# A graph network's last half: layer input added by TensorE, scaling split over two engines, h in one piece, new ranks

## The chip, the cores and the metric

One of the eight cores of a Trainium2 chip runs the kernel. A core has TensorE (matrix products into PSUM), VectorE, ScalarE and GpSimd (which work on SBUF, the first two on PSUM too), and SyncE, whose queue issues most of the transfers. In the profile they are PE (PEld for its weight loads), DVE, ACT, POOL and SP. Each engine takes its own instructions in program order; semaphores hold an instruction until what it reads is there. The metric is the device time of one execution in microseconds, median of three runs; less is better.

## What is computed

Sixteen images of 1024 nodes with 128 features (`x`), and one symmetric 0/1 matrix `adj`. A graph attention layer and a residual norm, then five steps of a gated graph network and another residual norm:

```python
# layer 0
h = x @ others_weight
e = leaky(u1[idx1] + u2[idx2])                 # one logit per pair
att = softmax(where(adj > 0, e, NEG_BIG), axis=1)
x = layernorm(x + att @ h + x @ self_weight)
# layer 1, five steps from h = x
m = adj @ h                                    # in and out matrix are the same
u = h @ u3.T
z = sigmoid([m, m] @ w3.T + b3 + u)
r = sigmoid([m, m] @ w4.T + b4 + u)
hv = tanh([m, m] @ w5.T + b5 + (r * h) @ u5.T)
h = (1 - z) * h + z * hv
# and the end
out = layernorm(x + h)                         # x: what entered layer 1
```

## The kernel before

**Tiles and stages.** An image's state lies transposed, features on the partitions and nodes along the row, in two halves of 512 nodes (`hT`, half 0 and 1). Images are taken in pairs, 0 and 1 up to 14 and 15. `layer0(b)` makes an image's layer input `y0`, stores a copy in DRAM (`yd`) for the end, and starts `hT`. `messages(q, s, k)` multiplies a pair with the adjacency matrix in step `s`: every operand is split into a high and a low part in a rounded fp32 format (`split`, L603 on ScalarE and L607 on VectorE), and each part multiplied (`product`, L615). Most steps share seven block products between the pair's two images; the first three steps of the first pair and the last three of the last pair are "plain" (`PLAIN`), image by image.

**A step of a gate.** `gates(b, s, soon)` handles both halves `e`: the product of `u3` with h (L1186), its copy (L1189), the products for r and z added in PSUM (L1196), their activations (L1199, a tanh from which the sigmoid is made), r times h (L1206), two products for the new value (L1212, L1213), tanh (L1221), and three VectorE instructions: hv minus h (L1224), times z (L1227), h (L1230). `pieces(b, s)` says in how many column pieces the part from the tanh on is done: 2 of 256 columns in the last step of the last image, otherwise 1 of 512.

**The end of an image.** `leave(b, s)` follows. After the last step each half is turned back to nodes on partitions: for the last three images by TensorE (`transposes`, L565, four 128x128 transposes), for the others by VectorE and transfers. The layer input comes back from DRAM (L1286), VectorE adds it (L1297), and `layernorm` does the rest: VectorE takes the statistics in four pieces of 128 (L521, L523), GpSimd makes 1/sqrt(var + eps) by a power (L527, L528), and then there are two forms. The long form has GpSimd make a bias too (two more instructions, L533 and L534 or L536 and L537) and ScalarE scale (L542, four instructions). The short form has VectorE subtract and multiply (L548, four instructions). The short form is used for the last image and for the second half of the image before it. Images 0 to 13 are stored through GpSimd's queue, the last two through SyncE's (L1317).

**The order of the work.** No loop sets it. Each piece of work is entered with `plan.add(engine, length, rank, ...)`, with what it reads and writes. `Plan.order()` plays the plan through once, before the kernel is built: an engine that is free takes the ready piece of lowest rank for which the tiles are free. A piece is ready when those before it have ended plus a lag by engine (`LAG`), and `CARE` ns more where VectorE or ScalarE feeds TensorE. Lengths on VectorE and ScalarE count 1.1 times (`MARGIN`). What comes out is emitted as it stands, so that ranks and lags decide the order of the instructions and nothing at run time.

A rank is mostly `rank_of(b, s)`: 10 for each pair, 4.2 for each step, and `LATER` for the last image in its plain steps. To this comes an offset by kind of work out of the table `D`: `pu`, `u`, `pr`, `pz`, `r`, `pv`, `z`, `hv`, `h` for the parts of a step, `m` for copies of messages, `tr` for turning back, `o`, `ln`, `out` for the end. `rank0(b)` with `l1` to `l8` is the same for the parts of layer 0: `l1` projections, `l2` row sums, `l3` scaled operands, `l4` products, `l5` turning, `l6` norm, `l7` and `l8` what follows.

**The start.** While `adj` is loaded TensorE runs up to 120 filler transposes (L419, rank 9000). Then come the projections of images 0 and 1 (L652), the row sums of the exponentials (L807, VectorE), the scaled operands (L856 ScalarE, L862 VectorE) and the attention products (L615 into `ps_acc_po`). For images 4 to 7 the product of `x` with the residual weights is made early (L455, "ahead", copied by L458 and stored). From image 2 on a row of exponentials goes through DRAM and comes back spread over all partitions (`pb`, L701 and L708).

Of the kernel before, what the change touches and what calls it, by code (L numbers as in the profile page):

```python
# [13 lines left out]
ALU = mybir.AluOpType  # L14
AX = mybir.AxisListType

P = 128
# [3 lines left out]
STEPS = 5  # L21
# [4 lines left out]
LOW, HIGH = -20.0, 100.0  # L26
TINY = 1e-30
PLAIN = {(0, 0), (0, 1), (0, 2), (7, 2), (7, 3), (7, 4)}
LATER = 3
AHEAD = range(4, 8)  # L30
LATE = 3001
TURNED = {(0, 0), (0, 1), (7, 2), (7, 3)}
# [3 lines left out]
class Plan:  # L36
# [5 lines left out]


    MARGIN = 1.1
    CARE = 200
    SAME = {"PE": 0, "DVE": 60, "ACT": 60, "POOL": 60, "SP": 2500, "DMA": 0}
    LAG = {"PE": 250, "DVE": 150, "ACT": 170, "POOL": 200, "SP": 2500, "DMA": 2400}

# [25 lines left out]
    def order(self):  # L74
# [14 lines left out]
        while events:  # L89
# [13 lines left out]
            while more:  # L103
                more = False
                for engine, queue in ready.items():
# [3 lines left out]
                    while queue:  # L109
# [3 lines left out]
                        if all(free[t[0]] > 0 for t in new):  # L113
# [6 lines left out]
                            for u in users[i]:  # L120
# [3 lines left out]
                                if ops[u][0] == "PE" and engine in ("DVE", "ACT"):  # L124
                                    lag += self.CARE
                                at[u] = max(at.get(u, 0), now + length + lag)
# [11 lines left out]
def kernel(  # L138
# [51 lines left out]
    nc = tc.nc  # L190
    B = x_t.shape[0]
# [15 lines left out]
    ident = const.tile([P, P], F32, tag="ident", name="ident")  # L207
# [10 lines left out]
    def exact(pools):  # L218

        def pool(name, bufs, space=None):  # L220
# [34 lines left out]
            "rstd": (3, [P, 2, 4], F32, None),  # L255
            "D": (6, [P, HALF], F32, bass.MemoryType.DRAM),
            "X": (24, [P, HALF + 16], F32, bass.MemoryType.DRAM),
# [9 lines left out]
        def T(t, dtype=None, shape=None):  # L267
            if t not in tiles:
                _, sh, dt, _ = kinds[t[0]]
                tiles[t] = places[t[0]].tile(  # L270
                    shape or sh, dtype or dt, tag=t[0], name="_".join(map(str, t)).replace("-", "n")
                )
            return tiles[t]
# [8 lines left out]
        def chunks(ap):  # L282

            return ap.rearrange("p (b c i) -> p c b i", b=4, c=4)

        plan = Plan({tag: k[0] for tag, k in kinds.items()})

        R, F, TR, V, A = 233, 858, 109, 605, 640

        def pe(*a, **k):  # L290
            plan.add("PE", *a, **k)

        def dve(*a, **k):
            plan.add("DVE", *a, **k)
# [4 lines left out]
        def sp(*a, **k):  # L299
            plan.add("SP", *a, **k)  # L300


        D = dict(m=-0.2, pu=1.4, u=0.8, pr=0.8, pz=1.4, r=1.7, pv=1.2, z=1.3, hv=-0.6, h=1.2, tr=1.6, o=5.0, ln=2.9)
        D.update(out=4.8, l1=-9, l2=-4, l3=-3, l4=-4, l5=-6, l6=-2.5, l7=-1, l8=-2)

        def on_pe(b, what):

            return b < 2 and what in ("y", "b") or b >= B - 3 and what == STEPS - 1 or (b // 2, what) in TURNED

        def plain(q, s):  # L310

            return (q, s) in PLAIN

        def rank_of(b, s):
            return 10 * (b // 2) + 4.2 * s + (LATER if b == B - 1 and plain(b // 2, s) else 0)

        def rank0(b):
            return 10 * (b // 2) - 1 * (1 - b % 2) + -1.0

        def sign(b):  # L320

            return 1 if b % 2 else -1
# [17 lines left out]
        def early_loads():  # L340
# [28 lines left out]
            writes=[(boot, "early"), (ws, "early"), (x0, "early"), (("xt", 1), "early"), *((t, "early") for k in staged for t in k)],  # L369
# [190 lines left out]
        def transposes(src, read, t, rank, cs=range(4), part=0):  # L560


            def emit():
                for j in cs:
                    nc.tensor.transpose(T(t)[:, j * P : (j + 1) * P], src()[:, j * P : (j + 1) * P], ident)  # L565

            pe(len(cs) * TR, rank, emit, reads=[*read, (("ident",), 0)], writes=[(t, part)])

        def turn(t, src, read, rank):


            def emit():
                nc.vector.transpose(T(t).rearrange("p (b c i) -> p b c i", b=4, c=4), turned(src()))

            dve(V, rank, emit, reads=read, writes=[(t, 0)])
# [49 lines left out]
        def layer0(b):  # L625

            first = rank0(b) - (60 if b == 0 else 0)
            rank = first + D["l1"]
            xt, hx, pb, u, us, uu, ud = (
# [147 lines left out]

            rank = first + D["l2"]

# [19 lines left out]

            rank = rank0(b) + D["l2"]  # L800
            junk = ("junk", b)
# [42 lines left out]
            if b == 0:  # L844
                own_weights()
            rank = rank0(b) + D["l3"]
            size = 1 if b == 0 else 4
# [317 lines left out]

        def pieces(b, s):

            return 2 if b == B - 1 and s == STEPS - 1 else 1

        def gates(b, s, soon):  # L1170
            rank = rank_of(b, s)
# [4 lines left out]
            for e in range(2):  # L1176
# [40 lines left out]
                for i in range(n):  # L1217
# [23 lines left out]
                    dve(length, rank + D["h"], times_, reads=[(hv, 1, i), (z, 1)], writes=[(hv, 2, i)])  # L1241
                    dve(length, rank + D["h"], h_, reads=[(hv, 2, i)], writes=[(hT, e) if n == 1 else (hT, e, i)])

        def leave(b, s):

            rank = rank_of(b, s)
            hT = ("hT", b)
            for g in range(2):

                def h(g=g):  # L1250
                    return T(hT)[:, g * HALF : (g + 1) * HALF]

                k, d = ("T", b, s, g), ("X", b, s + 1, g)
                if s < STEPS - 1 and on_pe(b, s):
                    t = ("ps", "t", b, s, g)
                    transposes(h, [(hT, g)], t, rank + D["tr"])
                    split(
                        ("blk", b, "h", s + 1, g),
                        lambda t=t: T(t).rearrange("p (c a j) -> p c a j", c=4, a=4),
                        [(t, 0)],  # L1260
                        rank_of(b, s + 1),
                    )
                    continue
                if s < STEPS - 1:
                    turn(k, h, [(hT, g)], rank + D["tr"])
                    away(k, d, rank + D["tr"])
                    continue

                t = ("ps", "t", b, s, g)
                n = pieces(b, s)  # L1270
                done = [(hT, g)] if n == 1 else [(hT, g, i) for i in range(n)]
                if on_pe(b, s):
                    for i in range(n):
                        transposes(h, [done[i]], t, rank + D["tr"], range(4 * i // n, 4 * (i + 1) // n), i)
                else:
                    t = ("F", b, s, g)
                    turn(k, h, [(hT, g)], rank + D["tr"])
                    away(k, d, rank + D["tr"])
                    back(d, t, rank + D["o"])


                o, yd = ("y0" if b == B - 1 else "o", b, "o", g), ("yd", b, g)
                sp(
                    450,
                    rank + (D["o"] if b < B - 1 else 0),
                    lambda o=o, yd=yd: nc.sync.dma_start(T(o).rearrange("p c d -> p (c d)"), T(yd)),  # L1286
                    reads=[(yd, 0), (hT, g) if b < B - 1 else (("m", b, s, 0), 0)],
                    writes=[(o, "y")],
                    lag=2300,
                )  # L1290
                for i in range(n):

                    def last(i=i, t=t, o=o, flat=on_pe(b, s)):
                        cs = slice(4 * i // n, 4 * (i + 1) // n)
                        x = T(o)[:, cs, :].rearrange("p c (a j) -> p c a j", a=4)
                        v = T(t).rearrange("p (c a j) -> p c a j", c=4, a=4) if flat else chunks(T(t))
                        nc.vector.tensor_tensor(x, v[:, cs], x, ALU.add)  # L1297

                    dve(V / n, rank + D["o"], last, reads=[(t, i), (o, "y")], writes=[(o, "raw", i)])

                def at(j, o=o):
                    return T(o)[:, j, :]

                layernorm(
                    ("o", b),
                    g,
                    rank + D["ln"],
                    [(o, "raw", i) for i in range(n)],
                    at,
                    at,  # L1310
                    (o, 0),
                    sign(b),
                    b == B - 1 or b == B - 2 and g,
                )

                def out_(o=o, g=g, by=nc.gpsimd if b < B - 2 else nc.sync):
                    by.dma_start(out[b].rearrange("(c p) d -> p c d", p=P)[:, 4 * g : 4 * g + 4, :], T(o))  # L1317

                if b < B - 2:
                    plan.add("POOL", 900, rank + D["out"], out_, reads=[(o, 0)], writes=[((o, "sent"), 0)], lag=2600)  # L1320
                else:
                    sp(450, rank + D["out"], out_, reads=[(o, 0)])


        def look_at(i):
# [53 lines left out]
        for i in range(2 * NC):  # L1379
# [6 lines left out]
            reads=[  # L1386
                *((("seen",), b, k) for b in range(B) for k in range(2)),
                *((("count",), i) for i in range(2 * NC)),
                (("bad",), 0),
                (("bad",), 1),  # L1390
            ],
            writes=[(("rstd", "ends"), 0)],
# [6 lines left out]
            reads=[(("ps", "t", "flag"), 0)],  # L1399
            writes=[(("flag",), 0)],  # L1400
# [208 lines left out]
    with ExitStack() as pools:  # L1609
        exact(pools)  # L1610
# [51 lines left out]
```

## Time and profile before

| | us |
|---|---|
| median of 3 runs | 1460.12 (1458.28 to 1460.99) |
| the profiled execution | 1457.82 |
| its span | 1456.0 |

Busy time by engine, in parts of the end of the span (from the view by stretches of time):

| stretch, us | TensorE | VectorE | ScalarE | GpSimd |
|---|---|---|---|---|
| 1431 to 1436 | 5.00 | 2.72 | 3.42 | 2.84 |
| 1436 to 1441 | 5.00 | 3.40 | 3.19 | 0.84 |
| 1441 to 1446 | 1.81 | 5.00 | 0.84 | 0.00 |
| 1446 to 1451 | 0.00 | 3.78 | 0.00 | 2.63 |
| 1451 to 1456 | 0.00 | 0.00 | 0.00 | 0.00 |

In the order of time, the last instructions of the last image are: its last gate product at 1440.04, tanh in pieces from 1439.38 to 1441.94, three VectorE instructions for each of four pieces, two transposes for each piece (1441.50 to 1445.62), the adds, the statistics of half 0 (1445.04) and half 1 (1446.40), GpSimd twice two instructions (1446.26 and 1447.70), the scalings (1447.65 and 1449.19), and the two stores (issued from 1448.79 on).

The profile gives start and duration of each instruction; matmul ends are modelled, so that a group's duration is some 0.16 us longer than its spacing. Busy shares are of the span. The chain of waits is of no use here: it ends after three pieces.

### The profile page before, as it was taken

Reading aid. Unit: us, or ns where it says so; the run is one execution under the profiler, and the core shown is the slowest. Engines: PE = TensorE matmul, PEld = TensorE weight load, DVE = VectorE, ACT = ScalarE, POOL = GpSimd, SP = SyncE. Lnnn points to the kernel's source line nnn. Section 1 sums busy time; section 2 is a strip of 40 time slices with the busy share of each in tenths; the row PEclk is TensorE's granted clock in tenths of the full one; section 3 lists DMA queues with packets and bytes.
Section 4 is the critical chain, followed back from the end, with each engine's and each line's share of the span. In section 5 each row is a group of like instructions: output and inputs, shape, how many; then the busy total and the mean of one; then the engine's idle time right before and its main releaser. Section 6 shows DMA issues by size and latency. Waiting matters only on the chain. (4 is left out here: it accounts for less than half of the span.)

```text
span 1456.0 us, 17810 instructions
## 1 busy us (share of the span) xinstructions
PE 1437.2 (99%) x5020; PEld 899.1 (62%) x5020; DVE 1166.5 (80%) x2769; ACT 896.2 (62%) x1786; POOL 196.7 (14%) x320
## 2 busy tenths in 40 slices
PE   9999999999999999999999999999999999999996
PEld 7666666666666666665666566665666656556663
DVE  6886789979898788978888688887889876776445
ACT  5655665666656765756756676566665666664643
POOL 0202000112111120112201120020210112000201
PEclk9999999999999999999999999999999999999998
DMA  7305434554335543454334543455433553223201
GB/s 258 128 27 152 145 95 138 157 183 131 95 116 153 160 130 94 137 153 131 99 110 133 150 142 84 116 147 171 110 100 104 141 162 110 60 71 87 72 0 31
DMA packets 188032, 174.20 MB, mean 120 GB/s; under 512 B 34239, under 2 KB 137366, under 8 KB 187926
## 3 DMA queue, kind: packets, MB, share of 16 engines
q1 hardware_dynamic: 182562, 156.41, 37.9%
q0 software_dynamic: 4800, 15.73, 3.3%
q8 instruction: 41, 0.67, 0.2%
q10 hardware_dynamic: 564, 0.85, 0.2%
q14 instruction: 65, 0.53, 0.1%
HBM read 95.68 MB, written 77.24 MB: 119 GB/s over the span
## 5 line engine op out<-in xcount | busy, mean ns | idle before, releaser
L1212 PE MATMUL ps_g_v<-m,wm 128*128 128x512 f32 x320 | 163.4, 592 | 0.0
L1213 PE MATMUL ps_g_v<-r,u5h 128*128 128x512 f32 x320 | 163.4, 592 | 0.0
L1196 PE MATMUL gz<-m,wm 128*128 128x512 f32 x320 | 158.8, 592 | 0.0
L1196 PE MATMUL ps_g_r<-m,wm 128*128 128x512 f32 x320 | 158.6, 593 | 0.2
L1186 PE MATMUL ps_g_r<-hT,u 128*128 128x512 f32 x320 | 151.8, 592 | 0.0
L1206 DVE SCALAR_TENSOR_TENSOR r<-r,hT 128x512 f32<-128x512 f32 x160 | 108.8, 685 | 51.8 <-ACT r L1199 51.1
L615 PE MATMUL ps_acc_a<-tab,blk_s 128*128 128x512 f32 x544 | 144.6, 407 | 0.0
L1199 ACT ACTIVATE r<-ps_g_r,bh 128x512 f32<-128x512 f32 x160 | 109.5, 687 | 49.6 <-PE ps_g_r L1196 47.3
L1224 DVE TENSOR_TENSOR hv<-hv,hT 128x512 f32<-128x512 f32 (+1 forms) x162 | 109.7, 679 | 37.2 <-ACT hv L1221 36.2
L615 PE MATMUL ps_acc_po<-adj,blk 128*128 128x512 f32 x512 | 136.9, 415 | 0.3 <-DVE blk L862 0.3
L1199 ACT ACTIVATE z<-gz,bh 128x512 f32<-128x512 f32 x160 | 109.8, 687 | 24.3 <-PE gz L1196 23.6
L615 PEld LDWEIGHTS ps_acc_a<-tab,blk_s 128*128 128x128 f32 x544 | 100.8, 188 | 31.5 <-issue 6.2
L615 PEld LDWEIGHTS ps_acc_po<-adj,blk 128*128 128x128 f32 x512 | 95.7, 188 | 33.3 <-issue 9.4
L1189 ACT COPY gz<-ps_g_r 128x512 f32<-128x512 f32 x160 | 91.4, 572 | 34.8 <-PE ps_g_r L1186 33.3
L1227 DVE SCALAR_TENSOR_TENSOR hv<-z,hv 128x512 f32<-128x512 f32 (+1 forms) x162 | 108.1, 671 | 1.5 <-ACT z L1199 0.7
L1230 DVE SCALAR_TENSOR_TENSOR hT<-hv,hT 128x512 f32<-128x512 f32 (+1 forms) x162 | 108.0, 671 | 1.2
L1213 PEld LDWEIGHTS ps_g_v<-r,u5h 128*128 128x128 f32 x320 | 60.6, 189 | 76.7 <-issue 61.6
L1196 PEld LDWEIGHTS gz<-m,wm 128*128 128x128 f32 x320 | 60.6, 190 | 75.7 <-issue 75.6
L607 DVE TENSOR_TENSOR blk_s<-G,blk_s 128x512 fp32r<-128x512 f32 x136 | 91.3, 681 | 13.6 <-ACT blk_s L603 13.2
L527 POOL TENSOR_SCALAR rstd_y<-mv_y 128x4 f32<-128x4 f32 x32 | 13.2, 413 | 650.3 <-DVE mv_y L523 649.6
L603 ACT CAST blk_s<-G 128x512 fp32r<-128x512 f32 x136 | 82.0, 618 | 27.5 <-DVE G L1077 26.3
L615 PE MATMUL ps_acc<-adj,blk_h 128*128 128x512 f32 x384 | 97.5, 406 | 0.3 <-DVE blk_h L607 0.3
(189 smaller groups left out, 2586.7 us busy)
## 6 DMA issues: line engine op xcount, KB each, us to landing
G<-X SPq DMA_DIRECT2D x140, 256.0 KB
X<-T SPq DMA_DIRECT2D x552, 64.0 KB
yd<-y POOLq DMA_DIRECT2D x32, 256.0 KB, 3.0
o_o<-yd SPq DMA_DIRECT2D x30, 256.0 KB
D_y<-T_y SPq DMA_DIRECT2D x112, 64.0 KB
F_y<-D_y SPq DMA_DIRECT2D x28, 256.0 KB
X<-y SPq DMA_DIRECT2D x28, 256.0 KB
D_b<-T_b SPq DMA_DIRECT2D x112, 64.0 KB
```

Of the source, the lines that this page charges most:

```text
L607: lambda: nc.vector.tensor_tensor(half(1), src(), half(0), ALU.subtract),
L615: nc.tensor.matmul(T(bank), T(blk)[:, k, c, :], right(c), start=(first and i == 0), stop=(last and i == len(terms) - 1), skip_group_check= ...
L1186: nc.tensor.matmul(T(pr), u3, h(), start=True, stop=True)
L1189: nc.scalar.copy(T(pz), T(pr))
L1196: nc.tensor.matmul(T(p_), wm[:, j, :], T(m), start=False, stop=True, skip_group_check=True)
L1199: nc.scalar.activation(T(t), T(p_), AF.Tanh, bias=bh[:, j : j + 1], scale=0.5 * sg)
L1206: lambda r=r, h=h: nc.vector.scalar_tensor_tensor(T(r), T(r), 1.0, h(), ALU.add, ALU.mult),
L1212: nc.tensor.matmul(T(pv), wm[:, 2, :], T(m), start=True, stop=False)
L1213: nc.tensor.matmul(T(pv), u5h, T(r), start=False, stop=True)
L1224: nc.vector.tensor_tensor(T(hv)[:, w], T(hv)[:, w], h()[:, w], ALU.subtract)
L1227: nc.vector.scalar_tensor_tensor(T(hv)[:, w], T(z)[:, w], 1.0, T(hv)[:, w], ALU.add, ALU.mult)
L1230: nc.vector.scalar_tensor_tensor(h()[:, w], T(hv)[:, w], 0.5, h()[:, w], ALU.mult, ALU.add)
```

## The change

In the last step of the last two images `leave` hands over to a new function `end`, and the rest of `leave` loses its cases for them. For the very last half (image 15, half 1) TensorE first copies the layer input into PSUM by a product with the identity and then adds h's four transposed blocks to it, as plain products with the identity; statistics and the short form then read PSUM. For the other three halves the transposes and VectorE's add stay, and the long form with ScalarE is used. `pieces` always gives 1, so the last image's tanh, its three VectorE instructions and the adds work on whole halves. The layer inputs of image 14 are loaded as early as those of image 15. `LATER` goes from 3 to 1.5 and `CARE` from 200 to 400; eight entries of `D` differ; and layer 0 of images 2 and 3 has its rank lowered by 6.

```diff
-    LATER = 3
+    LATER = 1.5
-    CARE = 200
+    CARE = 400
-        D = dict(m=-0.2, pu=1.4, u=0.8, pr=0.8, pz=1.4, r=1.7, pv=1.2, z=1.3, hv=-0.6, h=1.2, tr=1.6, o=5.0, ln=2.9)
-        D.update(out=4.8, l1=-9, l2=-4, l3=-3, l4=-4, l5=-6, l6=-2.5, l7=-1, l8=-2)
+        D = dict(m=-0.4, pu=1.4, u=1.2, pr=0.8, pz=1.4, r=1.7, pv=1.0, z=1.3, hv=-0.6, h=1.6, tr=1.6, o=5.8, ln=2.9)
+        D.update(out=4.4, l1=-9, l2=-4, l3=-3, l4=-4, l5=-7, l6=-1.5, l7=-1, l8=-2)
         def rank0(b):
-            return 10 * (b // 2) - 1 * (1 - b % 2) + -1.0
+            return 10 * (b // 2) - 1 * (1 - b % 2) + -1.0 - 6 * (b // 2 == 1)
         def pieces(b, s):
-            return 2 if b == B - 1 and s == STEPS - 1 else 1
+            return 1
+        def end(b, s, g, h, rank):
+            hT, t = ("hT", b), ("ps", "t", b, s, g)
+            o, yd = ("y0" if b == B - 1 else "o", b, "o", g), ("yd", b, g)
+            sp(450, rank, lambda: nc.sync.dma_start(T(o).rearrange("p c d -> p (c d)"), T(yd)),
+                reads=[(yd, 0), (("m", b, s, 0), 0)], writes=[(o, "y")], lag=2300)
+            def y_():
+                nc.tensor.matmul(
+                    T(t), ident, T(o).rearrange("p c d -> p (c d)"), start=True, stop=False, skip_group_check=True
+                )
+            def h_():
+                for j in range(4):
+                    c = slice(j * P, (j + 1) * P)
+                    nc.tensor.matmul(T(t)[:, c], h()[:, c], ident, start=False, stop=j == 3, skip_group_check=True)
+            if (b, g) == (B - 1, 1):
+                pe(F, rank + D["tr"] + 0.1, y_, reads=[(o, "y"), (("ident",), 0)], writes=[(t, "y")])
+                pe(F, rank + D["tr"], h_, reads=[(hT, g), (t, "y"), (("ident",), 0)], writes=[(t, 0)])
+                sum_ = (t, 0)
+            else:
+                transposes(h, [(hT, g)], t, rank + D["tr"])
+                def add_():
+                    x = T(o).rearrange("p c d -> p (c d)")
+                    nc.vector.tensor_tensor(x, T(t), x, ALU.add)
+                dve(V, rank + D["o"], add_, reads=[(t, 0), (o, "y")], writes=[(o, "raw")])
+                sum_ = (o, "raw")
+            def src(j):
+                return T(t)[:, j * P : (j + 1) * P] if sum_[0] == t else T(o)[:, j, :]
+            def dst(j):
+                return T(o)[:, j, :]
+            layernorm(("o", b), g, rank + D["ln"], sum_, src, dst, (o, 0), sign(b), b == B - 1 and g == 1)
+            sp(450, rank + D["out"],
+                lambda: nc.sync.dma_start(out[b].rearrange("(c p) d -> p c d", p=P)[:, 4 * g : 4 * g + 4, :], T(o)),
+                reads=[(o, 0)])
...
+                if b >= B - 2:
+                    end(b, s, g, h, rank)
+                    continue
...
-                layernorm(
-                    ("o", b), g, rank + D["ln"],
-                    [(o, "raw", i) for i in range(n)], at, at, (o, 0), sign(b),
-                    b == B - 1 or b == B - 2 and g,
-                )
+                layernorm(("o", b), g, rank + D["ln"], (o, "raw"), at, at, (o, 0), sign(b))
```

## The prediction

> **What bounds the kernel now.** I read the page's busy shares first, then busy time by stretches of 40 us, then what TensorE waited for, then the order of time at both ends.
>
> ```profile
> PE 1437.2 (99%) x5020; PEld 899.1 (62%) x5020; DVE 1166.5 (80%) x2769; ACT 896.2 (62%) x1786; POOL 196.7 (14%) x320
> ```
>
> TensorE is busy 99% of the span. A busy TensorE can still hide gaps, so I checked the spacing: a 128x512 fp32 product starts 0.86 us after the one before it throughout, and the stretches show no holes in the middle (columns: PE, PEld, DVE, ACT, POOL busy time, clock, DMA share, GB/s).
>
> ```profile
> 0.00:40.00 40.00, 36.42 (x233) 28.62 (x234) 25.94 (x92) 20.09 (x56) 0.81 (x9) 1.00 0.73 242
> 40.00:80.00 40.00, 38.59 (x181) 28.31 (x180) 33.27 (x121) 24.38 (x64) 10.33 (x20) 1.00 0.41 133
> 80.00:120.00 40.00, 40.00 (x144) 25.53 (x144) 36.09 (x109) 24.68 (x58) 2.50 (x5) 1.00 0.12 34
> ...
> 160.00:200.00 40.00, 39.68 (x147) 25.39 (x146) 33.12 (x82) 23.03 (x44) 0.00 (x0) 1.00 0.38 103
> ...
> 1440.00:1456.00 16.00, 2.81 (x11) 0.99 (x9) 9.74 (x40) 1.06 (x3) 2.63 (x4) 0.68 0.18 54
> ```
>
> From 80 to 1440 us the missing TensorE time is 0.6 us in all (0.32 of it at 160 to 200). So the middle is TensorE's sum of work, which the change hardly touches, and time can be won or lost in three places: the first 60 us, a stall that a new order puts into the middle, and the last 16 us. In the first 60 us the stall that the new ranks can reach is the one around 50 us (order of time: start, duration, engine, line, in brackets the idle time before and what ended it):
>
> ```profile
> 47.56 1.51 ACT L542 ACTIVATE y<-ps_t_y,rstd_y 128x128 f32<-128x128 f32 x4
> 50.45 1.38 PE L565 MATMUL ps_t_b<-ident,y 128*128 128x128 f32 x4 [1.00 <-ACT y L542]
> 54.64 1.90 PE L615 MATMUL ps_acc_po<-adj,blk 128*128 128x512 f32 x7 [0.33 <-DVE blk L862]
> ```
>
> From 48.6 to 56.4 us the starts of TensorE's instructions leave 3.2 us unused (7.8 us, in which stand 8 transposes of 0.11 and 16 products of 0.234). The end:
>
> ```profile
> 1440.04 1.02 PE L1213 MATMUL ps_g_v<-r,u5h 128*128 128x512 f32 x2
> 1445.18 0.44 PE L565 MATMUL ps_t<-ident,hT 128*128 128x128 f32 x2 [1.23 <-DVE y_o L1297]
> 1447.18 0.36 DVE L523 BATCH_NORM_AGGREGATE mv_o<-stats_o 128x2 f32<-128x6 f32 x4
> 1448.12 1.04 POOL L528 TENSOR_TENSOR rstd_o<-rstd_o,mhalf 128x4 f32<-128x4 f32 x1
> 1449.19 1.12 DVE L548 TENSOR_SCALAR y_o<-y_o,mv_o,rstd_o 128x128 f32<-128x128 f32 x4 [0.43 <-POOL rstd_o L528]
> ```
>
> TensorE leaves its last gate product at E = 1440.04 + 0.86 = 1440.90. VectorE then works through 256-column pieces to 1447.54, GpSimd needs 1.6 us, VectorE's last scaling ends at 1450.31, that is E + 9.41. The store takes the other 5.7 us to 1456.0.
>
> [...] back to back the pieces start every 0.34 us and whole ones every 0.61, so halving buys overlap and costs some VectorE time. [...] the trace shows each engine in program order, so a late instruction delays all behind it. [...] a 128-column transpose here takes one record of 0.11 us, the plain fp32 product of the same size (L750) two records of 0.11, so the ratio in this trace is two.
>
> **The change, part by part.** Times in the tail are relative to E; the order on each engine is that of the changed kernel as built.
>
> 1. The layer input of the very last half goes through TensorE: one 128x512 fp32 product with the identity (as L1186: 0.86 us) stands between the last two h products and the gates. TensorE's line from the last adjacency product to E is full before (1431.8 to 1440.9 for ten products of 0.86 and one transposition group of 0.44), so nothing hides it: **+0.86**. Its input is loaded well before (the two loads are issued at 1365 in the profile), and it waits for nothing.
>
> 2. ScalarE gets the scaling of both halves of image 14 and the first of image 15 (L542, 4 pieces, 1.56 us) in place of VectorE's 1.11. Order on ScalarE: r, r, z, scale 14/0, z, tanh 0, scale 14/1, tanh 1, scale 15/0. The second z is available at -3.23 but starts after scale 14/0, at -1.9; tanh 0 then starts at -1.27 where its bank was ready at -1.52; scale 14/1 runs -0.64 to 0.92, so tanh 1 waits from 0.20 to 0.92. GpSimd's rstd for both halves (4 instructions each, 2.3 us as at 45.95 to 48.28) is done by -2.6, so these scalings wait for nothing else.
>
> 3. h in one piece. Dependent VectorE steps of 512 columns start 0.73 to 0.79 apart (1414.49, 1415.22, 1416.01). Half 0: -0.54, 0.19, 0.98 to 1.67. VectorE is in that chain until 0.98 + 0.6, so tanh 1, ready at 1.61, costs only a few hundredths: minus, times of half 1 at 1.66 and 2.4; then the layer-input add of half 0 at 3.0 (transposed by 2.35); h of half 1 at 3.6 to 4.3. Statistics of half 0: 4.25 to 5.4.
>
> 4. The last half: four plain fp32 products onto the layer input, 8 records of 0.11 = 0.87, from 4.37, readable at 5.45; statistics from PSUM (0.8 + 0.36, as L521 on ps_t_y) to 6.6. The add of 0.39 and the wait for it are gone. But GpSimd now computes four instructions for half 0 (5.47 to 7.5: 1.4 for the first two as at 1446.26 to 1447.61, then 0.3 and 0.24) where the short form had two, and the last half's two stand behind them: 7.5 to 8.95 instead of 6.7 to 8.15. That is 0.8 us of a new wait, 1.1 if the four take 2.3. VectorE scales from PSUM 9.0 to 10.1. Against 9.41: **+0.7**. The store of the last half is the same; that of half 0 (after ScalarE, 9.2) is now 0.9 ahead of it instead of 1.6, and both still overlap only in part: 0 to 0.2, taken as 0.
>
> 5. Ranks. Up to the product at 35.34 us TensorE's list is the same but for where four filler transposes stand. After it, image 2's eight projections come first (1.78 us), ending the list before the transposition of y at 48.7 instead of 48.6. There the wait for L542 is longer, since L542 now stands behind all six copies of the ahead products: 49.5 to 51.05, then the split (0.6 ScalarE, 0.65 VectorE) before the first adjacency product, 51.65 and 52.3. The list as far as 55.86 holds 4.18 us of work in 7.14: 3.0 us lost against 3.2: **-0.2**. From there I followed VectorE's list to 97 us against TensorE's: image 1's split is ready at 74.15 where it is wanted at 74.4, the next at 79.2 against 80.2, r of image 0 at 94.2 against 96.4. VectorE is nearly without a gap, but TensorE isn't held.
>
> 6. CARE 400 makes the planner put 0.2 us more between VectorE or ScalarE and TensorE. It can't gain more than the 0.6 us missing in the middle; bounds -0.6 and, if a new order meets a late transfer, several us. In the built order of the last 100 us no split, gate or copy has less TensorE work before its use than in the old one by a margin that matters (r to its product: 3.4 us at least, 1.7 needed). I take **-0.4**.
>
> Sum: 0.86 + 0.7 - 0.2 - 0.4 = **+0.96**. The profiled execution took 1457.82 (1456.0 of span), 2.3 below the median of the three runs, 1460.12; the difference is carried to the median: 1461.1.
>
> **Rivals.** (A) The early stretch holds TensorE: slower. The changed VectorE list has a row sum over image 2's exponentials (L807) ahead of image 0's split. Its operand comes through a copy at 43.4, a store, and a 512 KB broadcast behind two other transfers on SP's queue; if that lands after 49.8 us, VectorE stops and each us passes to TensorE, which has nothing else at 51. For: VectorE is busy 36 of 40 us at 80 to 120, and my comparison leaves it 0.2 to 2 us of lead to 97 us. Against: the planner allowed 3 us for that transfer, as my timing does. With 4 us more it gives 0.96 + 3.8 = +4.8, 1464.9. It decides from about 2 us on. (B) All goes well: the stall at 50 us vanishes (-3.2), the middle's too (-0.6), and the tail ends at 9.3 because GpSimd's halves fall apart: 0.86 - 0.1 - 3.2 - 0.6 = -3.0, 1457.1. Against: the longer wait for L542 is in the list. (C) The end's add on TensorE costs more than it says: TensorE rests 2.2 us before the last products, and the clock is 0.50 in the profile once it has rested (1446 to 1451). At half speed they take 1.74: +0.9, 1462.0.
>
> **Numbers.** 0.2% is 2.9 us, about what a measurement of this kernel can tell from no change. Forecast 0.56 (own range 1459.3 to 1463), A 0.30, B 0.08, C 0.06. With the forecast's edges: faster 0.10, same 0.57, slower 0.33. Low 1457.4 leaves some 0.08 under it, high 1466 about 0.12 over it.
>
> **What would show it.** In the profile after: TensorE's last gate product some 0.4 to 0.9 us later than 1440.0; a scaling of ScalarE between the last two tanh; GpSimd's last pair waiting behind four; VectorE's last scaling about 10.1 us behind E; 39.7 or more of 40 us of TensorE in each stretch from 80 to 1440. Wrong would be: a wait of TensorE for VectorE, or of VectorE for the broadcast, of over 1 us between 49 and 130 us (A), no stall near 50 us (B), or a tail that ends under 9.4 or over 11 us after E.

## The result

| | before | after |
|---|---|---|
| median, us | 1460.26 (18 runs) | 1465.32 (18 runs) |
| the profiled execution, us | 1457.82 | 1464.59 |
| its span, us | 1456.0 | 1462.4 |
| TensorE's last gate product ends (E) | 1440.90 | 1447.04 |
| VectorE's last scaling ends | E + 9.41 | E + 10.29 |

After against before: ratio 1.0033, 95% interval 1.0024 to 1.0041. The change makes the kernel slower by some 5 us. The range on record holds 1465.3, but not through its sum: that gave 1461.1, with an own range that ends at 1463, and the likeliest outcome, no difference that can be measured, did not come.

The question is where the 6.1 us that E comes later are from. First the view by stretches of time of the kernel after (columns as before: PE, PEld, DVE, ACT, POOL busy time, clock, DMA share, GB/s):

```profile
80.00:120.00 40.00, 40.00 (x147) 25.66 (x146) 35.45 (x105) 24.04 (x59) 6.73 (x14) 1.00 0.36 106
120.00:160.00 40.00, 38.52 (x150) 24.74 (x149) 25.92 (x58) 24.34 (x48) 3.61 (x6) 1.00 0.43 132
...
240.00:280.00 40.00, 39.72 (x135) 24.38 (x134) 35.49 (x91) 27.73 (x59) 6.49 (x10) 1.00 0.44 127
...
320.00:360.00 40.00, 39.23 (x133) 23.37 (x132) 35.58 (x86) 29.86 (x58) 9.26 (x14) 1.00 0.49 139
360.00:400.00 40.00, 38.60 (x124) 22.92 (x124) 33.27 (x76) 26.35 (x56) 7.42 (x6) 1.00 0.34 93
```

The first column after the comma is TensorE. From 80 to 1440 us it misses 4.3 us of its time (0.6 before), 3.9 of them in these stretches. The 6.1 us are made up of 0.86 for the added product, 0.7 in the first 28 us, where TensorE waited 2.47 us for an input (`r_x`) instead of 1.2, and, by difference, some 4.6 in the middle, of which the busy time shows 3.7. The wait for `r_x` is between 1.7 and 2.6 us in the profiles of ten of the thirteen kernels in the table below, so that the 0.7 is the luck of the one profiled execution of before and not the change. That execution was 2.4 us under its kernel's median, the one of after only 0.7 under its own. So some 1.7 us of what the two profiles show is luck of this kind. The view of what each engine waited for shows who holds TensorE in the middle (kernel after; engine, tile and line, what it waited for: us in all, times, longest):

```profile
PE ps_g_v L1213 <- DVE r L1206: 1.5, 2, 1.0
PE ps_acc_a L615 <- ACT m L1135: 1.4, 1, 1.4
...
PE ps_g_r L1196 <- ACT gz L1189: 0.6, 1, 0.6
```

None of these has anything to do with the new end. Followed in the order of time (start, duration, engine, in brackets the idle time before and what ended it), the first goes to VectorE and SyncE's queue (kernel after):

```profile
133.79 0.43 DVE L1386 TENSOR_SCALAR junk_look<-look 128x512 f32<-128x512 f32 x1 [4.58 <-DMA look<-in_adj_dram]
135.43 6.36 SPq L1379 DMA_DIRECT2D look<-in_adj_dram  x2
140.27 0.43 DVE L1386 TENSOR_SCALAR junk_look<-look 128x512 f32<-128x512 f32 x1 [5.32 <-DMA look<-in_adj_dram]
141.35 0.69 DVE L1206 SCALAR_TENSOR_TENSOR r<-r,hT 128x512 f32<-128x512 f32 x1
142.09 1.12 PE L1213 MATMUL ps_g_v<-r,u5h 128*128 128x512 f32 x2 [0.97 <-DVE r L1206]
```

`look` is a block of `adj` that is loaded anew to be compared with 0 and 1, work that nobody waits for. But VectorE takes its instructions in order: while it waits 5.32 us for `look`, r stands behind it, and TensorE's product behind r. The second goes to GpSimd (kernel after):

```profile
363.21 3.77 POOL L527 TENSOR_SCALAR rstd_o<-mv_o 128x4 f32<-128x4 f32 x1 [2.25 <-DVE mv_o L523]
363.21 0.67 DVE L1224 TENSOR_TENSOR hv<-hv,hT 128x512 f32<-128x512 f32 x1
...
366.21 0.67 DVE L607 TENSOR_TENSOR blk_x<-G,blk_x 128x512 fp32r<-128x512 f32 x1
366.82 0.69 DVE L573 STREAM_TRANSPOSE T<-hT 128x512 f32<-128x512 f32 x1
369.23 1.65 ACT L542 ACTIVATE o<-o,rstd_o 128x128 f32<-128x128 f32 x4 [4.88 <-POOL rstd_o L534]
370.78 0.56 ACT L1135 COPY m<-ps_acc_a 128x512 f32<-128x512 f32 x1
371.40 2.13 PE L615 MATMUL ps_acc_a<-tab,blk_s 128*128 128x512 f32 x8 [1.40 <-ACT m L1135]
```

GpSimd's addition on 128x4 numbers takes 0.23 us in the tail (at 1454.59, below) and 3.77 here: it begins together with the first of six VectorE instructions without a gap, each with two operands in SBUF, and ends 0.1 us after the last of them, when VectorE goes on to a transposition with one operand. That the row on VectorE holds it is read from these times; no run takes the row away. The kernel before has such a hold too: one GpSimd instruction (L536) takes 3.17 us at 681 us beside five of these on VectorE, and TensorE is busy there without a gap (14.00 of 14 us from 676 to 690). There the hold alone costs nothing; what stands behind it decides. ScalarE's scaling waits 4.88 us for the result, the copy of a message stands behind the scaling, and TensorE waits for the copy. The third (0.6 at 321 us) is a gate copy behind a split that waits 2.64 us for its load.

The end of the kernel after:

```profile
1446.18 1.02 PE L1213 MATMUL ps_g_v<-r,u5h 128*128 128x512 f32 x2
1446.21 1.64 ACT L542 ACTIVATE o_o<-o_o,rstd_o 128x128 f32<-128x128 f32 x4
1451.14 2.08 PE L1265 MATMUL ps_t<-ident,hT 128*128 128x128 f32 x8 [1.87 <-DVE hT L1230]
1453.25 0.89 DVE L521 BATCH_NORM_STATS2 stats_o<-ps_t 128x6 f32<-128x128 f32 x4 [1.11 <-PE ps_t L1265]
1454.59 0.23 POOL L527 TENSOR_SCALAR rstd_o<-mv_o 128x4 f32<-128x4 f32 x1 [0.42 <-DVE mv_o L523]
1455.97 1.36 DVE L548 TENSOR_SCALAR y_o<-ps_t,mv_o,rstd_o 128x128 f32<-128x128 f32 x4 [1.54 <-POOL rstd_o L528]
```

The tail is as long as forecast (10.29 for 10.1), but a slower clock has a part in it: the eight last records (TensorE's instructions as the profile counts them) take 2.08 us at a clock of 0.50, and VectorE waits 1.11 us for them. The kernel after with CARE at 200 (see the experiments) has the same tail with the clock at 1.00:

```profile
1449.50 1.16 PE L1265 MATMUL ps_t<-ident,hT 128*128 128x128 f32 x8 [1.87 <-DVE hT L1230]
1453.98 1.37 DVE L548 TENSOR_SCALAR y_o<-ps_t,mv_o,rstd_o 128x128 f32<-128x128 f32 x4 [2.12 <-POOL rstd_o L528]
```

Its last gate product ends at 1445.39, so its last scaling at E + 9.96. Five kernels have this tail with the slow clock (eight records in 2.07 or 2.08 us) and end at 10.29 or 10.30. With the slower clock this tail is 0.33 us longer.

### The profile page after: what moved, and what is told of

Read it like the earlier page. It is cut to its first block, busy times and chain, and to the rows that moved or that the text cites. A ratio compares the mean times of both kernels' runs of the same rounds, so it can differ in the third digit from the quotient of the medians.

```text
span 1462.4 us, 17792 instructions
## 1 busy us (share of the span) xinstructions
PE 1440.0 (98%) x5026; PEld 901.1 (62%) x5026; DVE 1163.3 (80%) x2752; ACT 896.7 (61%) x1792; POOL 205.2 (14%) x323
## 4 chain that ended last, share of the span: by engine, by line
PE 88%; DMA 4%; DVE 3%; ACT 1%; issue 1%; SPq 1%; POOL 1%; POOLq 0%; DVEq 0%; ACTq 0%
PE ps_acc_a L615 17%; PE ps_g_r L1186 9%; PE ps_g_r L1196 9%; PE ps_g_v L1213 8%; PE gz L1196 8%; PE ps_g_v L1212 8%; PE ps_acc_c L615 8%; PE ps_acc_po L615 8%; PE ps_acc L615 5%; PE gz L615 4%; PE ps_g_ph L652 2%; DMA G<-X 1%; PE ps_acc_px L919 1%; PE ps_acc_po L933 1%; SPq L583 1%
## 5 line engine op out<-in xcount | busy, mean ns | idle before, releaser
L1224 DVE TENSOR_TENSOR hv<-hv,hT 128x512 f32<-128x512 f32 x160 | 109.4, 685 | 55.9 <-ACT hv L1221 55.2
L615 PE MATMUL ps_acc_a<-tab,blk_s 128*128 128x512 f32 x544 | 147.8, 413 | 1.5 <-ACT m L1135 1.4
L1230 DVE SCALAR_TENSOR_TENSOR hT<-hv,hT 128x512 f32<-128x512 f32 x160 | 108.1, 678 | 2.3
L1227 DVE SCALAR_TENSOR_TENSOR hv<-z,hv 128x512 f32<-128x512 f32 x160 | 108.0, 677 | 1.9 <-ACT z L1199 0.9
L527 POOL TENSOR_SCALAR rstd_y<-mv_y 128x4 f32<-128x4 f32 x32 | 16.7, 522 | 649.2 <-DVE mv_y L523 647.8
L615 PE MATMUL ps_acc<-adj,blk_h 128*128 128x512 f32 x384 | 103.4, 417 | 0.6 <-ACT blk_h L603 0.3
L573 DVE STREAM_TRANSPOSE T<-hT 128x512 f32<-128x512 f32 x138 | 96.4, 701 | 2.3 <-DMA X<-T 2.0
```

What stands on the lines that cost most here:

```text
L615: nc.tensor.matmul(T(bank), T(blk)[:, k, c, :], right(c), start=(first and i == 0), stop=(last and i == len(terms) - 1), skip_group_check= ...
L1224: nc.vector.tensor_tensor(T(hv)[:, w], T(hv)[:, w], h()[:, w], ALU.subtract)
L1227: nc.vector.scalar_tensor_tensor(T(hv)[:, w], T(z)[:, w], 1.0, T(hv)[:, w], ALU.add, ALU.mult)
L1230: nc.vector.scalar_tensor_tensor(h()[:, w], T(hv)[:, w], 0.5, h()[:, w], ALU.mult, ALU.add)
```

## The experiments

Theories at the outset, as the expectations name them. **M**: the loss is in the middle, where the new order holds TensorE. **T**: the end itself costs it. **S**: each order that the planner finds is a draw, with stalls where an in-order engine's next instruction happens to wait for a late transfer or a blocked GpSimd, and the order of before was a good one. All ratios are to the kernel before, with 95% intervals; "missing" is what TensorE lacks from 80 to 1440 us in the profiled execution (length less busy time, summed over the stretches). "Half clock" counts the stretches ahead of the tail in which TensorE's granted clock was 0.50 in that execution. By estimate one lasts some 3.2 us: the mean clock is 0.96 over the 40 us that hold one (new end with the old ranks, first try, 0 to 40 us).

| kernel | median, us | ratio | missing, us | half clock |
|---|---|---|---|---|
| before | 1459.6 to 1460.4 | 1 | 0.6 | 0 |
| after | 1465.32 | 1.0033 (1.0024 to 1.0041) | 4.3 | 0 |
| new end, old ranks (first, second try) | 1460.98, 1461.08 | 1.0008 (0.9993 to 1.0023), 1.0012 (1.0003 to 1.0022) | 3.1, 2.2 | 1, 0 |
| new ranks and CARE, old end | 1474.56 | 1.0087 (1.0069 to 1.0105) | 11.1 | 2 |
| after, rank of images 2 and 3 as before | 1468.41 | 1.0043 (1.0028 to 1.0059) | 5.4 | 2 |
| after, planned lag 2300 instead of 2500 | 1476.55 | 1.0107 (1.0094 to 1.0121) | 11.9 | 3 |
| before, CARE 400 | 1473.07 | 1.0080 (1.0064 to 1.0096) | 9.8 | 4 |
| after, CARE 200 | 1463.14 | 1.0026 (1.0015 to 1.0037) | 2.3 | 1 |
| after, no look transfers | 1462.66 | 1.0015 (1.0007 to 1.0023) | 2.5 | 2 |
| after, 26 scalings later | 1470.40 | 1.0074 (1.0061 to 1.0087) | 10.1 | 0 |
| new end repaired, old ranks | 1459.85 | 1.0002 (0.9993 to 1.0011) | 2.5 | 1 |
| the same, both halves by TensorE | 1459.76 | 0.9998 (0.9988 to 1.0007) | 1.8 | 0 |

The last column is a cost that "missing" leaves out, because a TensorE at half clock counts as busy (the last eight records are 2.08 us of busy time in after at 0.50, and 1.16 with CARE 200 at 1.00). By estimate each such stretch costs half of its 3.2 us, 1.6. Between 60 and 1440 us there are eight, and each began with or shortly after the end of a rest of TensorE of 1.9 to 3.9 us; after the two rests of 2.5 and 2.6 us with 26 scalings later the clock stayed at 1.00. So a long stall was often paid for twice here. After itself has none, and its loss is the stalls alone.

### The end alone, twice

The changed kernel with the old values of the planner:

```diff
-LATER = 1.5
+LATER = 3
-    CARE = 400
+    CARE = 200
-        D = dict(m=-0.4, pu=1.4, u=1.2, pr=0.8, pz=1.4, r=1.7, pv=1.0, z=1.3, hv=-0.6, h=1.6, tr=1.6, o=5.8, ln=2.9)
+        D = dict(m=-0.2, pu=1.4, u=0.8, pr=0.8, pz=1.4, r=1.7, pv=1.2, z=1.3, hv=-0.6, h=1.2, tr=1.6, o=5.0, ln=2.9)
...
-            return 10 * (b // 2) - 1 * (1 - b % 2) + -1.0 - 6 * (b // 2 == 1)
+            return 10 * (b // 2) - 1 * (1 - b % 2) + -1.0
```

> The new end alone, with the old ranks, CARE and LATER. Theory M (the loss is a new order that holds TensorE between 60 and 1440 us): TensorE's deficit from 80 to 1440 us falls from about 4 us to about 1 us, the tail after TensorE's last gate product stays at about 10.2 us, the time is before + 0.9 to + 1.8. Theory T (the end itself costs what was lost): before + 4 to + 5. A third, theory S (any new plan falls at random into late transfers, the old one was a lucky draw): the deficit in the middle is 2 to 6 us here too, before + 3 to + 7.

The change also drops `lag=2300` from the reload of the layer inputs of images 0 to 13, so that the planner falls back on 2500. The second try puts it back (in `leave`, at that transfer):

```diff
                     writes=[(o, "y")],
+                    lag=2300,
                 )
```

> The new end alone, this time with TensorE's list exactly that of before but for the one added product: the first try also carried the missing lag of 2300 ns for the reload of the layer inputs, which moves the plan. If the end costs what the prediction said, before + 1.0 to + 1.8 (0.86 for the product, 0.7 to 0.9 in the tail); nothing more lost from 80 to 1440 us than before. If the end was the loss (theory T): before + 4 to + 5.

Measured: +1.2 and +1.8 us by the ratios. With the old ranks the lag changes nothing in the order on TensorE, VectorE and ScalarE, so the two are one order measured twice, and TensorE's list is that of before with one product more. T falls: the end costs 1.2 to 1.8 us, what the prediction made of it (0.86 + 0.7), though the first interval takes in 0. The missing time is a warning, though: 2.2 and 3.1 us in two executions of an order that lost 0.6 in before's profile (the stalls stand at 164 and 315 us in one, at 168 and 611 in the other). The 0.6 was a good execution, not the floor.

### The ranks alone

The kernel before, with the new `LATER`, `CARE`, `D` and `rank0`:

```diff
-LATER = 3
+LATER = 1.5
-    CARE = 200
+    CARE = 400
...
-            return 10 * (b // 2) - 1 * (1 - b % 2) + -1.0
+            return 10 * (b // 2) - 1 * (1 - b % 2) + -1.0 - 6 * (b // 2 == 1)
```

> The new ranks, CARE and LATER alone, with the old end (h in two pieces, layer input added by VectorE, two scalings of four on VectorE). Theory M: before + 2.5 to + 4, the deficit from 80 to 1440 us is 3 us or more. Theory T: before within 1 us.

Measured +12.7 us: M's place, and much more than its size. The order isn't that of after in the middle, since this kernel keeps the lag of 2300. That left one number to test.

### One planned number: 2300 instead of 2500

The changed kernel with the one line `lag=2300,` that the second try above adds, and nothing else.

> The changed kernel with 2300 ns instead of 2500 ns written into the plan as the lag of the reload of the layer inputs of images 0 to 13. No instruction is added, removed or resized; only the order that the plan finds differs. Theory S (each order is a draw, and stalls come where an engine's next instruction happens to wait for a late transfer or for GpSimd): the time moves by over 1.5 us to either side of the changed kernel's 1465.3, and the stalls of 140, 320 and 370 us stand elsewhere. Theory M in the form that the new ranks themselves are bad: within 1.5 us of 1465.3.

Measured +15.6 us against before, and some 11 against after, with the same instructions in another order. Its worst stall (kernel with the lag of 2300):

```profile
PE ps_acc_a L615 <- ACT m L1135: 7.9, 4, 3.9
...
537.76 0.34 SPq L591 DMA_DIRECT2D G<-X  x1
538.19 3.54 SPq L583 DMA_DIRECT2D X<-T  x4
543.03 0.62 ACT L603 CAST blk_x<-G 128x512 fp32r<-128x512 f32 x1 [6.35 <-DMA G<-X]
543.55 0.58 ACT L1135 COPY m<-gz 128x512 f32<-128x512 f32 x1
548.03 3.68 PE L615 MATMUL ps_acc_a<-tab,blk_s 128*128 128x512 f32 x8 [3.94 <-ACT m L1135]
```

The load of `G`, issued at 537.76, is there at 543.0, 5.3 us later; the planner counts on 2.4. ScalarE waits 6.35 us for it with the copy behind, and TensorE 3.9. Then the clock falls (its mean from 480 to 640 us is 0.99): the eight products from 548.03 on take 3.68 us, where eight of the same line and tiles took 2.12 at 541.12. S is shown in this form: with the new ranks and CARE, 200 ns in one number of the plan, and no change of the work, move the time by 11 us.

Up to the end this is, instruction for instruction on TensorE, VectorE, ScalarE and SyncE, the order of the ranks alone. So the four kernels part the change: ranks and CARE cost 12.7 us, the end some 3 more (1.0107 against 1.0087, the intervals overlap), and the dropped lag took 11 back.

### Which of the planner's numbers

The changed kernel without the lower rank of images 2 and 3:

```diff
-            return 10 * (b // 2) - 1 * (1 - b % 2) + -1.0 - 6 * (b // 2 == 1)
+            return 10 * (b // 2) - 1 * (1 - b % 2) + -1.0
```

> The changed kernel without the 6 taken from the rank of layer 0 of images 2 and 3. Theory M in its narrow form (it is the earlier work of images 2 and 3 that pushes the comparisons of the adjacency matrix and their transfers into a busy stretch at 120 to 150 us): the waits for the look transfers fall under 10 us in all, the time falls by 2 to 3 us. Theory S: another draw, the deficit moves elsewhere and the time is within 2 us of the changed kernel.

Measured 1.0043, some 1.5 us above after (3.1 by the medians, and the intervals overlap), its waits for look 16.0 us in all instead of 19.4. M in the narrow form falls; the stall moved (2.9 us at 167 us). Then `CARE`, on the kernel before alone:

```diff
-    CARE = 200
+    CARE = 400
```

> The kernel before with CARE at 400 instead of 200 and nothing else. The prediction's step 6 took this for a gain of at most 0.6 us: before - 0.6 to 0. Theory S: another draw of the order, TensorE loses 2 us or more in stalls between 80 and 1440 us, before + 2 to + 14.

Measured +11.7 us. VectorE shows the same kind of hold as in after, longer (kernel before with CARE 400):

```profile
162.50 7.12 SPq L1338 DMA_DIRECT2D look<-in_adj_dram  x2
168.09 0.43 DVE L1345 TENSOR_SCALAR junk_look<-look 128x512 f32<-128x512 f32 x1 [7.90 <-DMA look<-in_adj_dram]
```

A split for TensorE (L607) stands behind it and comes 3.3 us late. Last, the changed kernel with `CARE` back:

```diff
-    CARE = 400
+    CARE = 200
```

> The changed kernel with CARE back at 200 and nothing else: new end, new ranks. So far every order found with CARE at 400 was slower in the middle (by 3 to 14 us), and the one found with 200 was not. Theory C (CARE at 400 is what makes orders bad, the ranks do little): before + 1 to + 3, the end alone, and TensorE misses under 1.5 us between 80 and 1440 us. Theory S (any order that was not picked by measuring is worse than the picked one): before + 4 to + 15, with stalls of TensorE of over 3 us in all between 80 and 1440 us.

Measured +3.8 us (2.2 to 5.4), TensorE missing 2.3 us: between the two expectations. The missing time is that of the old order in its usual executions, as theory C has it; the time is 2 us above the end alone, but the intervals overlap. In the profiled executions 1.5 of these 2 us lie ahead of 52 us, where one stretch at half clock stands (mean clock 0.98 over the first 80 us); the end alone had that in one of its two profiles (0.96 over the first 40 us). Together: four orders with CARE at 400 miss 4.3 to 11.9 us, two with 200 miss 0.6 to 3.1. That speaks for CARE as a part of the loss. But in the changed kernel itself 200 gives back only 1.0 us, and the intervals overlap (1.0024 to 1.0041, 1.0015 to 1.0037). How much of the change's 5 us is due to CARE is not shown, and whether 400 makes orders worse by its nature or these were four bad draws stays open.

### The hold by look, in one order

The changed kernel with every instruction where it was, but the comparison reads the matrix that lies in SBUF:

```diff
-                lambda: nc.sync.dma_start(T(a), adj_t[c * P : (c + 1) * P, e * HALF : (e + 1) * HALF]),
+                lambda: None,
...
-                lambda: nc.vector.tensor_scalar(T(mask), T(a), 0.0, None, ALU.is_equal),
+                lambda: nc.vector.tensor_scalar(T(mask), here, 0.0, None, ALU.is_equal),
```

(`here` is the same block of `adj` in SBUF, also in the second comparison.)

> The changed kernel in the same order of instructions; the 16 comparisons of the adjacency matrix (L1379, L1386, L1372) read the matrix that lies in SBUF already instead of one loaded anew: same VectorE work, no transfer, no wait. Left out by it: the comparison of the input as it stands in DRAM. Theory M, with the look transfers as the cause at 120 to 150 us: TensorE's waits for r (L1206) at 140 and 147 us go, -1.5 us; the stalls at 320 and 370 us stay. If the waits of VectorE for these transfers are only idle time that would be spent on another wait, no change within 0.5 us.

Measured 1462.7, 2.7 us under after, and TensorE has 40.00 of 40 us at 120 to 160. The waits for r are gone, the stall at 370 us stayed; that at 320 went too, and one of 0.8 came at 339. The mechanism is shown; its worth is 1.5 us by the trace, and more by the times, though the two intervals (1.0024 to 1.0041, 1.0007 to 1.0023) only just do not meet. The edit also takes 16 transfers out of SyncE's queue; what that alone is worth was not measured.

### The hold by GpSimd, in one order

The changed kernel; after the plan is made, each scaling of an end norm goes two ScalarE instructions back:

```diff
-        return started
+        return postpone(started, ops, users)
...
+def postpone(started, ops, users):
+    for i in [i for i in started if ops[i][3].__name__ == "scale" and any(t[0] == "o" for t in ops[i][5])]:
...
+                started[a : act2 + 1] = [j for j in started[a : act2 + 1] if j != i] + [i]
```

> The changed kernel with every engine's list unchanged but ScalarE's, where 26 scalings of the end norms (L542, images 0 to 12) stand two instructions later. At 363 us GpSimd's first instruction of the norm (L527) takes 3.77 us while VectorE runs six instructions with two SBUF operands back to back; the scaling then waits 4.88 us for GpSimd with the copy of a message (L1135) behind it, and TensorE waits 1.40 us for that copy. If this chain is the cause: TensorE's wait of 1.40 us at 369 us goes, GpSimd's 3.77 us stays, and the time falls by 1.0 to 1.9 us below the changed kernel's 1465.3. If the copy was late by itself: the wait of 1.40 us stays and the time is within 0.4 us.

The local part came as expected, the time did not: 5 us slower than after. In this kernel, with the later scalings:

```profile
365.33 3.76 POOL L527 TENSOR_SCALAR rstd_o<-mv_o 128x4 f32<-128x4 f32 x1 [0.92 <-DVE mv_o L523]
366.77 0.59 ACT L1135 COPY m<-ps_acc_a 128x512 f32<-128x512 f32 x1 [0.96 <-PE ps_acc_a L615]
...
1226.93 0.34 SPq L1337 DMA_DIRECT2D o<-yd  x1
1229.71 0.69 DVE L1345 TENSOR_TENSOR o<-F,o 128x512 f32<-128x512 f32 x1 [4.28 <-DMA o<-yd]
```

GpSimd takes 3.76 us as before, the copy no longer waits for it, and TensorE's 1.40 us are gone. But a later scaling is a later store, `o` has two buffers, and so the reload of the next layer input is issued late: VectorE waits 4.28 us for it (1.33 at the same place in after) with r behind, and TensorE 2.6. A second stall of this kind, of 2.5 us, stands at 1373 us. No engine waits for the scalings directly; they set when a buffer comes free.

### Repairs of the end

In the order of before, the product for the layer input is held back until the last r is there, so that it stands behind the last gate product, and image 15's first half gets the short form:

```diff
-                pe(F, rank + D["tr"] + 0.1, y_, reads=[(o, "y"), (("ident",), 0)], writes=[(t, "y")])
+                pe(F, rank + D["tr"] + 0.1, y_, reads=[(o, "y"), (("ident",), 0), (("r", b, s, 1), 2)], writes=[(t, "y")])
...
-            layernorm(("o", b), g, rank + D["ln"], sum_, src, dst, (o, 0), sign(b), b == B - 1 and g == 1)
+            layernorm(("o", b), g, rank + D["ln"], sum_, src, dst, (o, 0), sign(b), b == B - 1)
```

> As the new end alone in the order of before, with two repairs: the product that brings the layer input into PSUM stands behind the last gate product, where TensorE rests, and the first half of the last image is scaled by VectorE in the short form, so that GpSimd has two instructions before the last half's two instead of four. The product's 0.86 us is then free, and the last scaling ends about 10.0 us after TensorE's last gate product instead of 10.25: before + 0.3 to + 0.8, about 1 us less than the new end alone. If the product wasn't exposed, or VectorE's extra scaling comes in the way of the last one: no better than the new end alone.

Measured +0.3 us (-1.0 to +1.6), 0.9 and 1.5 less than the two measurements of the end alone, though the intervals overlap. In the profile the last scaling follows at nearly the same distance from the last gate product (10.34 us, and 10.24 in the end alone), so what the two repairs gained is the product, which was exposed. The 10.0 forecast for the tail did not come; TensorE is slow again (end repaired; mean clock 0.56 from 1448 to 1451 us):

```profile
1447.99 1.76 PE L1265 MATMUL ps_t<-ident,hT 128*128 128x128 f32 x8 [1.81 <-DVE hT L1230]
```

Then both halves by TensorE:

```diff
-            if (b, g) == (B - 1, 1):
+            if b == B - 1:
```

> Order of before; in the last image both halves get their layer input from TensorE, in two products behind the last gate product, where TensorE rests; both are scaled by VectorE from PSUM. With respect to the tail with two repairs, VectorE's add (0.6 us, ahead of the last h) goes, and TensorE rests about 1 us instead of 1.8 before the last eight records, which then take 1.0 us instead of 1.76. The last scaling ends about 9.2 us after the last gate product instead of 10.3: about 1 us less than that kernel, before - 0.8 to + 0.2. If TensorE's slower clock in the tail comes from something other than its rest, 1.76 stays, and the gain is about 0.4.

The last scaling ends at 1451.65, 9.20 behind the last gate product at 1442.45, as expected (both halves by TensorE):

```profile
1446.37 1.16 PE L1265 MATMUL ps_t<-ident,hT 128*128 128x128 f32 x8 [0.96 <-DVE hT L1230]
1448.86 2.79 DVE L548 TENSOR_SCALAR y_o<-ps_t,mv_o,rstd_o 128x128 f32<-128x128 f32 x8
```

Eight records in 1.16 us after a rest of 0.96 us, against 1.76 after 1.81. That the shorter rest is the reason isn't shown: in after with CARE 200 the eight took 1.16 too, after 1.87. The time is before - 0.3 us (-1.8 to +1.0): the gain of 1.1 us in the tail is below what the measurement tells, and no version here beats the kernel before.

## Why the prediction was right and wrong

The sum was +0.96 us and +4.8 came by the ratio. The range held because its upper edge, 1466, left room for rival A; that A's 1464.9 is so near is chance, for the stall at 50 us that it rests on did not come.

1. *The product, +0.86*: right. It takes 0.86 of TensorE's full line; behind the last gate product it falls into TensorE's rest.
2. *ScalarE's scalings*: right. The scaling of 14/1 runs from 1446.21 to the last tanh at 1447.75, 0.71 after E (0.92 forecast).
3. *h in one piece*: right to 0.3: h of half 1 at 3.36 to 4.04 after E for 3.6 to 4.3.
4. *The last half, +0.7*: the size is right (10.29 for 10.1), the reason in part. In the profiled execution the clock after TensorE's rests was 0.50, rival C's mechanism, and VectorE waited 1.11 us; GpSimd's four instructions for half 0 were then done in time. At clock 1.00 (CARE 200) GpSimd's last pair waits 0.74 us behind the four, 0.8 forecast, and the end is at 9.96. In the end alone the eight records took 1.26 us in one execution and 2.07 in the other, and both ended at 10.24. Two limits of nearly one length stand beside each other, and C's 0.9 us shrank to 0.33. What was not seen: the stores end 5.1 us after the last scaling instead of 5.7, so that E to the end of the span grew by 0.3 only.
5. *The early stretch, -0.2*: right. Shifted by the 0.7 of the first wait, the products came at 52.32 and 53.05 where 51.65 and 52.3 had been worked out, and 3.05 us are lost for 3.0.
6. *CARE and the middle, -0.4*: this step failed. The new order's middle cost 4.6 us in the profiles and, by the ratios, some 3 to 3.6 (4.8 less the 1.2 to 1.8 of the end alone); CARE alone cost the kernel before 11.7 us. The step named the right danger as its bound ("if a new order meets a late transfer, several us") and then took the other side, on lists followed only to 97 us and over the last 100; the stalls stood at 140, 147, 320 and 369. It also took the 0.6 us missing in one profile for the most that a middle can lose or win, where the same order misses 1.8 to 3.1 in other executions. And the dropped `lag=2300` was not priced at all: in the new plan dropping it saves 11 us, in the old one it changes nothing. What the runs show in place of the gain is stalls behind two holders, transfers and a blocked GpSimd; which of the planner's numbers is to blame in the changed kernel stays open.

Rival A had the mechanism (VectorE's queue held by a late transfer ahead of what TensorE needs), with 30%, but looked for it at the broadcast of 50 us; it came at the look transfers from 120 us on, and with GpSimd as a second holder that the prediction had not considered.

## What to carry to other kernels

Where a planner fixes the order of in-order engines, a change of one of its numbers can be a new draw of all its stalls: price it by what other orders of the same kernel lose in the middle (0.6 to 11.9 us here), or compare several orders by measurement, and don't judge the middle by the order at both ends. Read the clock beside the busy time, for the half clock after a long stall (1.6 us each by the estimate above, after rests of 1.9 to 3.9 us) is not in it. Ahead of what the bounding engine waits for, put nothing that waits for a transfer or for GpSimd (5.32 and 4.88 us in after), not even work that nobody needs soon; and before moving such work back, look which buffer it frees.

## What was not expected of the hardware

- A 128x4 GpSimd addition takes 0.23 us in the tail, and 3.76 or 3.77 in five kernels (after, no look transfers, 26 scalings later, ranks alone, lag 2300) where the same six VectorE instructions with two SBUF operands follow each other without a gap. Beside five such instructions a GpSimd instruction of the kernel before took 3.17. That is some 0.6 us for each of them, the distance of their starts. Such a row alone doesn't do it: at 687.59 us of the kernel before the addition took 0.71 us within six of these without a gap. What makes the difference was not found.
- TensorE's clock fell in the tail of every kernel (to 0.50 from 1445.75 us on in before, from 1450.0 in after), and the rests alone do not say when. In after, rests of 1.41 and 1.87 us with 0.66 us of transpositions between them ended in a clock of 0.50 and twice the time for the products behind; with CARE 200 the same rests left 1.00 (2.08 and 1.16 us). The end alone, one order, gave 2.07 us in one execution and 1.26 in the other. Ahead of the half-clock stretches in the middle the shortest rest was 1.88 us, while rests of 2.5 and 2.6 us with 26 scalings later left the clock at 1.00. What sets the moment was not shown.
- VectorE's scaling of four 128x128 pieces takes 1.36 us when it reads PSUM (after) and 1.12 from SBUF (before).
- A 256 KB load (`G`) issued just ahead of four small stores of SyncE's queue was there after 5.3 us (kernel with the lag of 2300, DMA share 0.67 from 535 to 540 us), where the page of after gives a median of 2.8 for these loads. Why it took so long was not tested.
